# Feed-forward's second layer by 49 block products for 56, and token sums kept in one copy

## The chip, the cores and the metric

The kernel runs on one core of a Trainium2 chip. The metric is the device time in microseconds, as the median of several runs. The profile and trace come from one profiled execution, with its own time.

## The reference, cut to what matters

A gated cross-attention block with a feed-forward network is followed by a slot-pooling block with experts. Batch 8, 512 tokens, width 512. Everything is in 32-bit floats. The change touches the feed-forward network (hidden width 2048) and the preparation of its weights:

```python
xn = layer_norm(x, gamma)
...
h = xn @ Wff1
a, gate = (h[..., :ff_inner], h[..., ff_inner:])
out = out + jax.nn.silu(gate) * a @ Wff2
...
x = x + jnp.tanh(g_xattn[0]) * _L0_xattn_ref(...)
```

Per batch, `xn` (512 x 512) is multiplied by `Wff1` (512 x 4096), and the gated product (512 x 2048) by `Wff2` (2048 x 512).

## The kernel before, in words

Four stages follow one another: cross-attention, the feed-forward network, the expert stage, and the last attention over the slots. Engines run their instructions in the order in which the program issues them (`manual_schedule`), and the order is written out by hand. SP issues nearly all DMAs, and an instruction on its queue that waits for an engine holds up those behind it.

**Seven products for eight.** The feed-forward network multiplies matrices as two by two blocks with seven block products instead of eight, on sums and differences of the blocks. The first layer does this twice, one level inside the other: seven outer products (lists `FIRST`), each of seven inner ones (`INNER`), 49 small products in all. The second layer does it once (`SECOND`), with seven products of eight matmuls each, 56 in all.

**Weights.** The sums of weight blocks are made in cross-attention by the generator `combine_weights`. Its tile `wx` holds four rows of blocks and POOL adds them (L507, helper `op`); SP loads the raw blocks and stores the sums into the DRAM tiles `w1c` and `w2c`. The cross-attention loop runs over half-steps h = 0 to 133 and calls `next(combining, None)` once in each with h > 0 (L818); after the loop, `for _ in combining` would run what is left (L852). For each of two groups `sg`, four `first_layer` calls of 12 steps come before a `second_layer` of 16. In the second layer, ACT scales the raw weights by the gate `tg_x` (L559).

**The feed-forward loop.** k runs over K = 16 pieces of work, two per batch (b = k // 2, sg = k % 2). In each k, `first(k, e, at)` runs for e = 0 to 6 and at = 0 to 6: four matmuls of 128 x 128 x 128 (L1111), then sums out of PSUM by DVE or ACT. Such a step is called a slot here; 49 make a period. PSUM banks: Y (two, in turn), Q, X, R. `moved` copies or adds Y into X (at = 0), tb (at = 2), t_c (at = 4) or the result (at = 6). All these sums pass through `tt` (L933). A later step on Y must wait until Y has been moved out. POOL does part of the work from SBUF: V + Z in e = 5, W + Z and the multiplications of h in e = 6, then four sums of 1024 columns over the hidden blocks (`combine_hidden`, tile `hs`).

`second(k)` is a generator that runs one period behind, from slot 7 of period k + 1. It gives one matmul of 256 columns (L1027) after each slot, two after the one with at = 3, and its results leave PSUM by ops of 512 columns. At the end of the stage the second layer of k = 15 runs alone.

**Tokens.** `xc` holds two copies of the token blocks and their sums, 7 x 7 blocks of 128 columns: one for the batch at work, one for the next, loaded by `load_tokens` (L939) and summed on POOL by `inner_tokens` and `outer_tokens`. `settle(b)` takes statistics of a finished batch on DVE (L1064), normalises on POOL (L1071) and transposes on DVE (L1081). Jobs with a slot number are put into a dictionary by `later`.

**The edge between the stages.** In the last batch, the sums x_kept go out by POOL's queue (L731), the other stores by SP's. SP's first instructions of the feed-forward stage are `load_tokens(0)` and three `load_first` (L964).

## Time and profile before

| quantity | value |
|---|---|
| median of 3 runs | 2792.7 us (2792.15 to 2794.26) |
| the profiled execution | 2795.4 us, span 2793.6 us |
| granted TensorE clock | 0.996 |
| cross-attention | from the start to about 1031 us |
| feed-forward, k = 0 | 1031.9 to about 1077 us |
| feed-forward, 15 periods | about 1077 to 2097 us, 68.0 us each |
| second layer of k = 15 alone | 2097.4 to about 2126.5 us |
| PE busy in 1077 to 2097 | 1019.9 of 1020 us |
| DVE, ACT, POOL busy there | 473.1, 224.9, 565.2 us |

How to read it: an engine's busy time says how long it worked, not whether anything waited for it. In the timelines a row gives the start and the length in us, the engine, the line, the operation with output and inputs, and in brackets the idle time before it and what ended that. A PE row merges records that follow each other, and each 32-bit matmul has two records. Long rows overlap the next ones a little, since a matmul's end includes its way through the array. "L933" is the helper `tt`, so such rows are told apart by tile and shape.

### The profile page before, as it was taken

The page shows a single profiled execution, that of the slowest core. Times are in us where ns is not written, and L with a number is a line of the kernel's source. Part 1 is how long each engine was busy: PE and PEld are TensorE (multiplying, and loading weights), DVE is VectorE, ACT ScalarE, POOL GpSimd, SP SyncE. Part 2 cuts the span into 40 slices and gives each one's busy share as a digit, 9 for nine tenths or more (in the row PEclk, how much of TensorE's full clock was granted, in tenths as well). Part 3 has the DMA queues.
Part 4 walks back from the last instruction along what each step waited for, and adds up shares of the span by engine and source line. Part 5 has one row for each costly group of instructions (what it writes and reads, how often), then busy time and mean ns, then how long its engine had stood idle before and what let it go on. Part 6 is the DMA issues. An engine that isn't in the chain of part 4 may idle for free.

```text
span 2793.6 us, 45441 instructions
## 1 busy us (share of the span) xinstructions
PE 2721.9 (97%) x16826; PEld 1716.7 (61%) x16826; DVE 1529.4 (55%) x3412; ACT 934.4 (33%) x2029; POOL 1442.7 (52%) x1023
## 2 busy tenths in 40 slices
PE   9999999999999999999999999999999998899889
PEld 5333333333333459999999999999997544322233
DVE  7897978888787754444444444444454221111146
ACT  5555556555556542222222222222221222000033
POOL 6787878778787645355555565656552100000035
PEclk9999999999999999999999999999999999999999
DMA  7888878888887788777877787878789799999954
GB/s 233 271 247 239 255 233 244 245 248 238 242 257 218 237 267 314 263 263 257 298 276 287 267 303 250 303 260 307 240 284 350 283 426 423 410 426 427 426 200 153
DMA packets 262973, 794.01 MB, mean 284 GB/s; under 512 B 90912, under 2 KB 121152, under 8 KB 235104
## 3 DMA queue, kind: packets, MB, share of 16 engines
q1 hardware_dynamic: 261872, 788.61, 80.6%
q8 instruction: 134, 2.20, 0.3%
q0 software_dynamic: 640, 2.10, 0.2%
q14 instruction: 87, 0.71, 0.1%
q10 hardware_dynamic: 240, 0.40, 0.0%
HBM read 574.44 MB, written 83.36 MB: 235 GB/s over the span
## 4 chain that ended last, share of the span: by engine, by line
PE 84%; DMA 11%; DVE 3%; ACT 1%; SPq 1%; issue 1%; POOL 0%; DVEq 0%; ACTq 0%; POOLq 0%
PE Y L1111 14%; DMA wg<-in_L_ffn_e_Wg_dram 8%; PE Y L1027 8%; PE av L406 8%; PE sim L327 8%; PE op L420 7%; PE qp L310 7%; PE Z L1027 4%; PE Q L1111 3%; PE R L1111 3%; PE X L1111 3%; PE Q L1027 2%; PE out L1935 2%; PE p_wg L1740 1%; DMA w<-in_L_ffn_e_W_dram 1%; PE pl L1388 1%
## 5 line engine op out<-in xcount | busy, mean ns | idle before, releaser
L354 POOL TENSOR_SCALAR pr<-pr,rden 128x512 f32<-128x512 f32 x378 | 592.2, 1582 | 205.7 <-DVE rden L347 205.4
L341 ACT ACTIVATE pr<-pr,nmx 128x512 f32<-128x512 f32 x512 | 363.4, 711 | 383.2 <-DVE nmx L338 295.6
L1111 PEld LDWEIGHTS Y<-xc,w 128*128 128x128 f32 x3608 | 469.4, 192 | 24.8 <-DVE h L933 0.9
L1111 PE MATMUL Y<-xc,w 128*128 128x128 f32 x3608 | 473.5, 275 | 2.1 <-DVE top_first L933 0.6
L338 DVE CUSTOM_DVE_ANT_0 pr<-sim,bias 128x512 f32<-128x512 f32 x512 | 321.9, 684 | 39.0 <-PE sim L327 39.0
L369 DVE STREAM_TRANSPOSE turned<-pr 128x512 f32<-128x512 f32 x504 | 322.5, 682 | 9.7 <-DMA pT<-turned 1.7
L933 POOL TENSOR_TENSOR fv<-fv,fz 128x512 f32<-128x512 f32 x64 | 79.9, 1269 | 381.3 <-ACT fz L1126 362.5
L327 PE MATMUL sim<-kT,q 64*128 64x512 f32 x1024 | 255.5, 615 | 0.9 <-DVE nmx L338 0.9
L406 PE MATMUL av<-pT,v 128*64 128x512 f32 x1008 | 232.9, 604 | 1.2 <-issue 1.0
L420 PE MATMUL op<-wo,o 128*128 128x512 f32 x512 | 231.3, 594 | 1.4 <-ACT o L412 1.4
L310 PE MATMUL qp<-xnT,wq 128*128 128x512 f32 x496 | 229.3, 605 | 0.5 <-ACT o L412 0.5
L1027 PE MATMUL Y<-w,h 128*128 128x256 f32 x736 | 211.7, 382 | 0.8 <-DVE top_first L933 0.8
L933 DVE TENSOR_TENSOR top_first<-Y,fv 128x512 f32<-128x512 f32 x128 | 88.6, 692 | 183.0 <-PE Y L1111 179.0
L327 PEld LDWEIGHTS sim<-kT,q 64*128 64x128 f32 x1024 | 89.0, 186 | 160.2 <-issue 97.2
L310 PEld LDWEIGHTS qp<-xnT,wq 128*128 128x128 f32 x496 | 89.1, 189 | 135.0 <-issue 119.3
L420 PEld LDWEIGHTS op<-wo,o 128*128 128x128 f32 x512 | 93.5, 190 | 103.2 <-issue 97.1
L406 PEld LDWEIGHTS av<-pT,v 128*64 128x64 f32 x1008 | 67.8, 138 | 141.8 <-issue 118.2
L507 POOL TENSOR_TENSOR wx<-wx 128x512 f32<-128x512 f32 (+2 forms) x96 | 131.0, 1372 | 1.3
L1305 POOL MEMSET cwk<- 128x2048 f32 x1 | 1.8, 1805 | 247.7 <-PE p_w L1740 247.7
L1662 DVE TENSOR_SCALAR place<-tq,vec 128x512 f32<-128x512 f32 x32 | 24.0, 751 | 191.9 <-PE tq L1349 191.9
L1370 POOL TENSOR_SCALAR spr<-spr,ssums 128x512 f32<-128x512 f32 x16 | 25.1, 1571 | 189.1 <-DVE ssums L1369 184.0
L933 DVE TENSOR_TENSOR R<-Q,top_first 128x512 f32<-128x512 f32 x109 | 76.2, 700 | 83.0 <-ACT top_first L1118 78.3
(358 smaller groups left out, 4513.0 us busy)
## 6 DMA issues: line engine op xcount, KB each, us to landing
w<-w1c SPq DMA_DIRECT2D x112, 1792.0 KB, 8.0
w<-in_L_ffn_e_W_dram SPq DMA_DIRECT2D x64, 2048.0 KB, 16.6
pT<-turned SPq DMA_DIRECT2D x1008, 128.0 KB, 2.7
wg<-in_L_ffn_e_Wg_dram SPq DMA_DIRECT2D x32, 2048.0 KB, 27.5
w<-w2c SPq DMA_DIRECT2D x108, 512.0 KB, 8.4
w1c<-wx SPq DMA_DIRECT2D x56, 448.0 KB, 3.6
wq<-wq_kept SPq DMA_DIRECT2D x52, 256.0 KB, 4.8
xn<-in_x_dram SPq DMA_DIRECT2D x32, 256.0 KB, 3.4
```

The costliest lines, as they stand in the source:

```text
L310: nc.tensor.matmul(qp, lhsT=w[:, c, :], rhs=xnT[:, c, :], start=(c == 0), stop=(c == ND - 1))
L327: nc.tensor.matmul(sps[l, e], lhsT=qs[half * HP + l][r, t * P : (t + 1) * P], rhs=kT[r, :], start=True, stop=True,)
L338: nc.vector.tensor_tensor_reduce(pr, sps[l, e], bias, -XSCALE, LARGE, ALU.add, ALU.min, nmx)
L341: nc.scalar.activation(pr, pr, AF.Exp, bias=nmx, scale=-1.0, accum_out=dens[l][:, e : e + 1])
L354: nc.gpsimd.tensor_scalar(prs[l, e], prs[l, e], rden[:, e : e + 1], None, ALU.mult)
L369: nc.vector.transpose(turned[:, :, hd, :].rearrange("p (k j) c -> p k j c", k=4), pr.rearrange("p (j k c) -> p k j c", k=4, c=32),)
L406: nc.tensor.matmul(av[XD * e : XD * e + XD], lhsT=v[:, j, :], rhs=p5[:, j, :, :, e, :], start=(j == 0), stop=(j == NT - 1),)
L420: nc.tensor.matmul(op, lhsT=o[:, l, :], rhs=wo[:, half * HP + l, :], start=(l == 0), stop=(l == HP - 1),)
L507: nc.gpsimd.tensor_tensor(dst, a, b, kind)
L933: eng.tensor_tensor(dst, a, b, op)
L1027: nc.tensor.matmul(bank[:, n], lhsT=h_blocks(k)[pa][:, n, q], rhs=w[:, q], start=fresh[e] and i == 0, stop=True, skip_group_check=True,)
L1111: nc.tensor.matmul(bank[:, q * P : (q + 1) * P], lhsT=w[:, q, ia, :], rhs=x[:, pb, ib, :], start=at < 2 and q == 0, stop=True, skip_group_ ...
```

## The change

The second layer gets the inner level too: seven products of seven inner ones, 49, each of two matmuls of 128 columns. Its weights get the second level in cross-attention: `second_layer(sg, c)` is called twice per sg, with 12 steps each, and `first_layer` has 11 steps instead of 12. `w2c` and the buffers `w2` grow from 8 to 14 blocks of 128 columns per product. The inner sums of the hidden blocks are made on the fly by `combine_inner` into two buffers `gs`, on DVE, four slots ahead of their product; each inner step moves its own 128 columns out of PSUM, and the sums over outer products go to y by `sums`, mostly on POOL.

The tokens have one copy. A row of the next batch's blocks is loaded into the place of a row that the last piece of the batch has just used; `HOLD` says which row lies where, and the jobs' slots are written out by hand. Tiles change their places in SBUF, and a tile `spare` keeps the distance.

```diff
-    w2c = [keep.tile([P, 7 * 1024], F32, name=f"w2c_{sg}") for sg in range(SG)]
+    w2c = [keep.tile([P, 7 * 2 * 7 * P], F32, name=f"w2c_{sg}") for sg in range(SG)]
...
                 put(6, 1)
                 yield
-                yield
-
-            def load(sg, q):
...
-            def first_half(q):
-                w = pieces[q % 2]
-                op(w[:, 4], w[:, 1], w[:, 0], ALU.subtract)
-                op(w[:, 5], w[:, 3], w[:, 4], ALU.subtract)
-
-            def second_half(q):
-                w = pieces[q % 2]
-                op(w[:, 1], w[:, 3], w[:, 1], ALU.subtract)
-                op(w[:, 6], w[:, 2], w[:, 5], ALU.subtract)
...
-            def put_second(sg, q):
-                nc.sync.dma_start(
-                    w2c[sg].rearrange("p (o q d) -> q p o d", o=7, q=4)[q], pieces[q % 2]
-                )
...
-            def second_layer(sg):
-                for i in range(3 * 3 + 6):
...
+
+            def second_layer(sg, c):
+                def put(o, src):
+                    at = (2 * o + c) * 7 * P
+                    nc.sync.dma_start(w2c[sg][:, at : at + 7 * P], o_[src])
...
+                for f in range(2):
+                    for kk in range(2):
+                        nc.sync.dma_start(
+                            wx[:, 2 * f : 2 * f + 2, 2 * kk : 2 * kk + 2].rearrange(
+                                "p h d w -> p h (d w)"
+                            ),
+                            rows_[f, kk],
+                        )
+                yield
+                yield
+                for i in range(2):
+                    raw = wx[:, 2 * i : 2 * i + 2, 0:4].rearrange("p o i w -> p o (i w)")
+                    nc.scalar.activation(raw, raw, AF.Copy, scale=tg_x)
+                yield
+                op(i_[4], i_[1], i_[0], ALU.subtract)
+                op(i_[5], i_[3], i_[4], ALU.subtract)
+                yield
+                op(i_[6], i_[2], i_[5], ALU.subtract)
+                op(i_[1], i_[3], i_[1], ALU.subtract)
+                yield
+                for o in (0, 2, 3):
+                    put(o, o)
+                yield
+                yield
+                op(o_[0], o_[1], o_[0], ALU.subtract)
+                yield
+                put(4, 0)
+                op(o_[1], o_[3], o_[1], ALU.subtract)
+                yield
+                put(1, 1)
+                op(o_[3], o_[3], o_[0], ALU.subtract)
+                yield
+                put(5, 3)
+                op(o_[2], o_[2], o_[3], ALU.subtract)
+                yield
+                put(6, 2)
                 yield
 
             for sg in range(SG):
                 for q in range(4):
                     yield from first_layer(sg, q)
-                yield from second_layer(sg)
+                for c in range(2):
+                    yield from second_layer(sg, c)
 
...
-        xc = [f1.tile([P, 7, 7, P], F32, name=f"xc_{i}") for i in range(2)]
+        xc = f1.tile([P, 7, 7, P], F32, name="xc")
+        HOLD = [[0, 1, 2, 3, 4, 5, 6]]
+        for _ in range(1, B):
+            r = HOLD[-1]
+            HOLD.append([r[0], r[2], r[4], r[5], r[3], r[1], r[6]])
...
+        V, W, Z = (sum_tile(n) for n in ("fv", "fw", "fz"))
         hidden_tile(1)
+        first_tile(1)
+        first_tile(2)
+        w2 = [f1.tile([P, 2, 7, P], F32, name=f"w2_{i}") for i in range(3)]
+        gs = [f1.tile([P, 4, 2, P], F32, name=f"g_{i}") for i in range(2)]
         first_tile(0)
         hidden_tile(0)
-        w2 = [f1.tile([P, 4, HD], F32, name=f"w2_{i}") for i in range(3)]
-        V, W = sum_tile("fv"), sum_tile("fw")
-        first_tile(1)
-        first_tile(2)
-        Z = sum_tile("fz")
         ys_[0] = f1.tile([P, 2, 2, D], F32, name="y_0")
         zs = [[f1.tile([P, HD], F32, name=f"z{i}_{n}") for n in range(2)] for i in range(2)]
+        f1.tile([P, 1664], F32, name="spare")
         hs = f1.tile([P, 3, 2, 4, P], F32, name="hs")
+        ub, u_c = (f1.tile([P, P], F32, name=n) for n in ("ub", "uc"))
...
-        tu, t22 = (top_first[:, i].rearrange("p (n d) -> p n d", n=2) for i in (4, 5))
+        V2, U2 = (top_first[:, i].rearrange("p (n d) -> p n d", n=2) for i in (4, 5))
...
-        Q2 = pf.tile([P, 2, HD], F32, name="Q2")
-        Y2 = pf.tile([P, 2, HD], F32, name="Y2")
-        Z2 = pf.tile([P, 2, HD], F32, name="Z2")
+        Q2, Y2, Z2 = (pf.tile([P, N], F32, name=n) for n in ("Q2", "Y2", "Z2"))
         Y0, Q, X, R = (pf.tile([P, N], F32, name=n) for n in ("Y0", "Q", "X", "R"))
-        others = ((Q, X, R), tuple(t.rearrange("p n d -> p (n d)") for t in (Q2, Y2, Z2)))
+        others = ((Q, X, R), (Q2, Y2, Z2))
...
-        def load_tokens(b):
-            src = xnT_kept[b].rearrange("p (c t n w) -> p c t n w", c=ND, t=2, n=2)
-            for c in range(ND):
-                kk, k2 = divmod(c, 2)
-                nc.sync.dma_start(
-                    xc[b % 2][:, 2 * kk : 2 * kk + 2, 2 * k2 : 2 * k2 + 2, :], src[:, c]
-                )
-
-        def inner_tokens(b, eng, o=slice(0, 4)):
-            x = xc[b % 2][:, o]
+        def load_tokens(b, o):
+            kk, t = divmod(o, 2)
+            src = xnT_kept[b].rearrange("p (c t m) -> p c t m", c=ND, t=2)
+            nc.sync.dma_start(
+                xc[:, HOLD[b][o], 0:4].rearrange("p (c n) w -> p c (n w)", c=2),
+                src[:, 2 * kk : 2 * kk + 2, t],
+            )
+
+        def inner_tokens(b, eng, *os):
+            r = sorted(HOLD[b][o] for o in os)
+            x = xc[:, r[0] : r[-1] + 1 : max(r[-1] - r[0], 1)]
...
-            x = [xc[b % 2][:, o].rearrange("p i n -> p (i n)") for o in range(7)]
+            x = [xc[:, HOLD[b][o]].rearrange("p i n -> p (i n)") for o in range(7)]
...
-            w = hb[0].rearrange("p t f n q w -> p (t f n q w)")[:, 1024 * i : 1024 * i + 1024]
-            return w.rearrange("p (q d) -> p q d", q=4)
+            w = w1[1 + i // 2].rearrange("p q i w -> p (q i w)")
+            n = 2 * 7 * P
+            return w[:, n * (i % 2) : n * (i % 2) + n].rearrange("p (c i d) -> p c i d", c=2, i=7)
...
-                o = SECOND[e][1]
+                o, n = SECOND[e][1], 2 * 7 * P
                 nc.sync.dma_start(
-                    second_weights(c),
-                    w2c[k % SG][:, o * 1024 : (o + 1) * 1024].rearrange("p (q d) -> p q d", q=4),
+                    second_weights(c).rearrange("p c i d -> p (c i d)"),
+                    w2c[k % SG][:, o * n : (o + 1) * n],
...
-        def second(k):
+        def inner_hidden(k, e):
+
+            a = h_blocks(k)[SECOND[e][0]]
+            a11, a12, a21, a22 = (a[:, n, 2 * c : 2 * c + 2] for n in range(2) for c in range(2))
+            a21_, s1, s2, s4 = (gs[(7 * k + e) % 2][:, j] for j in range(4))
+            return [a11, a12, a21_, a22, s1, s2, s4], a21
+
+        def combine_inner(k, e, eng):
+            (a11, a12, a21_, a22, s1, s2, s4), a21 = inner_hidden(k, e)
+            tt(eng, s1, a21, a22, add)
+            tt(eng, s2, s1, a11, sub)
+            tt(eng, a21_, a11, a21, sub)
+            tt(eng, s4, a12, s2, sub)
+
+
+
+        def second(k, e, at):
...
-            banks = (Y2, Q2, Y2, Z2, Y2, Z2, Y2)
-            fresh = (True, True, False, False, False, False, False)
-            v = nc.vector
-            for e, (pa, _) in enumerate(SECOND):
-                if k < K - 1:
-                    load_second(7 * k + e + 2)
-                w, bank = second_weights(7 * k + e), banks[e]
-                for i in range(8):
-                    q, n = divmod(i, 2)
-                    nc.tensor.matmul(
-                        bank[:, n], lhsT=h_blocks(k)[pa][:, n, q], rhs=w[:, q],
-                        start=fresh[e] and i == 0, stop=True, skip_group_check=True,
-                    )
-                    if i == 7:
-                        if e == 0:
-                            tt(v, Z2, Y2, y11, add)
...
-                        elif e == 6:
-                            tt(v, y21, Y2, y21, add)
-                    yield
+            v, s = nc.vector, nc.scalar
+            seed = (None, None, V2, y11, V2, y12, y21)[e]
+            to = (V2, U2, V2, y11, V2, y12, y21)[e]
+            if at == 0 and k < K - 1:
+                load_second(7 * k + e + 2)
+            left, w = inner_hidden(k, e)[0], second_weights(7 * k + e)
+            n = (7 * k + e) % 2
+            bank, both = (Q2, Y2)[n], Z2[:, n * HD : n * HD + HD]
+            Y, Q, X, R = bank[:, 0:P], bank[:, P : 2 * P], both[:, 0:P], both[:, P : 2 * P]
+            ia, ib = SECOND[at]
+            dst = (Y, Q, Y, X, Y, R, Y)[at]
+            for c in range(2):
+                nc.tensor.matmul(
+                    dst, lhsT=left[ia][:, c], rhs=w[:, c, ib], start=at == 0 and c == 0,
+                    stop=True, skip_group_check=True,
+                )
+
+            def moved(dst, n, d):
+                if seed is None:
+                    s.copy(dst, Y)
+                else:
+                    tt(v, dst, Y, seed[:, n, d * P : (d + 1) * P], add)
+
+            if at == 0:
+                moved(X, 0, 0)
+            elif at == 2:
+                moved(ub, 0, 1)
+                tt(v, R, Q, ub, add)
+            elif at == 4:
+                moved(u_c, 1, 1)
+                tt(v, to[:, 1, P : 2 * P], Q, u_c, add)
+            elif at == 5:
+                s.copy(to[:, 0], both)
+            elif at == 6:
+                moved(to[:, 1, 0:P], 1, 0)
+
+        def sums(k, e):
+            y = ys_[(k // SG) % 2]
+            y11, y12, y21, y22 = (
+                y[:, t, :, h * HD : (h + 1) * HD] for t in range(2) for h in range(2)
+            )
+            pairs = (
+                [(y11, V2)], [(y12, U2), (y22, U2)], [(y12, V2)], [], [(y21, V2), (y22, V2)], [], []
+            )[e]
+            return [lambda eng, y=y, a=a: tt(eng, y, y, a, add) for y, a in pairs]
...
-                    bank[:, q * P : (q + 1) * P], lhsT=w[:, q, ia, :], rhs=x[:, pb, ib, :],
+                    bank[:, q * P : (q + 1) * P], lhsT=w[:, q, ia, :], rhs=xc[:, HOLD[b][pb], ib],
...
-        load_tokens(0)
+        for o in range(4):
+            load_tokens(0, o)
...
+        def back(k):
+            at = 49 * (k + 1) + 7
+            for e in range(7):
+                later(at + 7 * e - 4, lambda e=e: combine_inner(k, e, nc.vector))
+                for i in range(7):
+                    later(at + 7 * e + i, lambda e=e, i=i: second(k, e, i))
+                for i, run in enumerate(sums(k, e)):
+                    eng = nc.vector if e == 4 and i == 0 else nc.gpsimd
+                    wait = (1, 8)[e == 4 and i == 1] + i
+                    later(at + 7 * e + 6 + wait, lambda run=run, eng=eng: run(eng))
+
+        RAW = {1: 0, 2: 1, 3: 3, 4: 2}
         hide(0)
-        seconds = []
+        back(0)
         for k in range(1, K):
             b, sg = divmod(k, SG)
             for e in range(7):
                 load_first(7 * k + e + 2)
+                if sg == 1 and b + 1 < B and e in RAW:
+                    load_tokens(b + 1, RAW[e])
+                if k == K - 1 and e > 4:
+                    for i in range(2):
+                        load_second(7 * k + 3 + 2 * (e - 5) + i)
                 for at in range(7):
                     first(k, e, at)
-                    for _ in range(2 if at == 3 else 1):
-                        if seconds and next(seconds[0], "end") == "end":
-                            seconds.pop(0)
-                            if seconds:
-                                next(seconds[0])
                     for run in jobs.pop(49 * k + 7 * e + at, []):
                         run()
-                if e == 0:
-                    seconds.append(second(k - 1))
-                if e == 0 and (sg == 0 or b == 0) and b + 1 < B:
-                    load_tokens(b + 1)
...
                     if b + 1 < B:
-                        for i, run in enumerate(
-                            inner_tokens(b + 1, nc.gpsimd) + outer_tokens(b + 1, nc.gpsimd)
-                        ):
-                            later(49 * k + 10 + 3 * i, run)
+                        inner = inner_tokens(b + 1, nc.gpsimd, 0, 1)
+                        inner += inner_tokens(b + 1, nc.gpsimd, 3, 2)
+                        outer = outer_tokens(b + 1, nc.gpsimd)
+                        runs = [*inner, outer[0], outer[1], outer[3], outer[2]]
+                        for i, run in zip((18, 20, 22, 24, 30, 32, 34, 36, 37, 45, 48, 54), runs):
+                            later(49 * k + i, run)
...
-        for _ in seconds[0]:
-            pass
-        for e in range(2, 7):
-            load_second(7 * (K - 1) + e)
-        for run in combine_hidden(K - 1, nc.vector):
-            run()
-        for _ in second(K - 1):
-            pass
+                back(k)
+        for slot in sorted(jobs):
+            for run in jobs.pop(slot):
+                run()
+        load_second(7 * (K - 1) + 2)
+        k = K - 1
+        outer = combine_hidden(k, nc.vector)
+        combine_inner(k, 0, nc.vector)
+        outer[0]()
+        outer[1]()
+        outer[2]()
+        outer[3]()
+        for e in range(7):
+            if e < 6:
+                combine_inner(k, e + 1, nc.gpsimd)
+            for at in range(7):
+                second(k, e, at)
+            for run in sums(k, e):
+                run(nc.vector)
```

## The prediction

> **What bounds the kernel now.** I read the page first, then the timeline of one feed-forward stretch, then DVE and POOL alone at places where both work on SBUF tiles, then SP and POOL at the end of cross-attention. On the page:
>
> ```profile
> PE 2721.9 (97%) x16826; PEld 1716.7 (61%) x16826; DVE 1529.4 (55%) x3412; ACT 934.4 (33%) x2029; POOL 1442.7 (52%) x1023
> PE 84%; DMA 11%; DVE 3%; ACT 1%; SPq 1%; issue 1%; POOL 0%; DVEq 0%; ACTq 0%; POOLq 0%
> ```
>
> PE is busy throughout and carries the chain. The feed-forward network runs from 1031.9 (first L1111) to 2126.5 us. The windows of it show PE busy 68.00 of 68.00 us in the periods (one per k), so there its time is the matmuls' pitch. The timeline of PE, from at=1 of a product on:
>
> ```profile
> 1603.76 1.05 PE L1111 MATMUL Y<-xc,w 128*128 128x128 f32 x8
> 1604.65 0.60 PE L1027 MATMUL Y<-w,h 128*128 128x256 f32 x2
> 1605.09 1.05 PE L1111 MATMUL X<-xc,w 128*128 128x128 f32 x8
> 1605.98 1.03 PE L1027 MATMUL Y<-w,h 128*128 128x256 f32 x4
> 1606.84 1.05 PE L1111 MATMUL Y<-xc,w 128*128 128x128 f32 x8
> ```
>
> A matmul is two records. Four 128-wide ones take 0.89 us of pitch (1604.65 - 1603.76), so 0.222 each; one 256-wide takes 0.44 (1605.09 - 1604.65). A slot is 1.33 us, the one with two second-layer matmuls 1.75; seven are 9.71, and seven of those the 68.0 of a period.
>
> **PE's gain.** Of each first-layer product's company, 8 matmuls of 256 columns (8 x 0.435 = 3.48) become 14 of 128 (14 x 0.222 = 3.11). That is 0.37 per product, 2.6 per period, 39 us over the 15 periods k = 1 to 15. All of it is on the path. A slot becomes 1.33 everywhere, a period 65.3. The first-layer matmuls and k = 0 stay.
>
> **DVE's new work.** DVE gets, per period, 28 sums of 256 columns in SBUF (`combine_inner`), some 34 ops of 128 columns out of PSUM, and one sum of 512 (y21); six ops of 0.69 go. Nearest rows: 128-wide with PSUM 0.288 (oT<-oT,y_tp), SBUF sums 0.28 at 128 and 1.22 at 1024 columns (hs), on whose line 256 columns take 0.42. So 11.8 + 9.8 + 0.7 - 4.1 = 18 us on top of about 31 busy in 65.3: enough in total. But the order is fixed. The four sums stand in slot 3 of each product, and the next slot's moves out of Y queue behind them. In the trace a tb sum starts 1.16 us after its slot does (Y at 1156.31, sum at 1157.47) and R follows to 1158.90; with two new 0.29 ops the four sums start 3.1 us after slot 2 does. PE's at=6 starts four slots (5.33) after slot 2 and waits for the t_c move (0.69). Room for the four sums: 5.33 - 3.1 - 0.69 = 1.5 us. They need 1.7 undisturbed: a stall near 0.1 each, 0.6 per period. In product 6 another 0.68 op (h<-X,h) is ahead of them, so there some 0.75. Every further us in the four sums is PE's, one for one.
>
> **POOL beside these sums.** This decides. Almost every DVE op of this stage now has one input in PSUM. Where DVE adds SBUF to SBUF beside POOL, at the start of the stage and at its end, the trace shows (DVE, then POOL; then POOL and DVE at 2100):
>
> ```profile
> 1031.87 0.29 DVE L933 TENSOR_TENSOR xc<-xc 128x128 f32<-128x128 f32 x1
> 1032.28 1.10 DVE L933 TENSOR_TENSOR xc<-xc 128x128 f32<-128x128 f32 x1
> 1033.62 0.70 DVE L933 TENSOR_TENSOR xc<-xc 128x128 f32<-128x128 f32 x1
> 1034.24 0.81 DVE L933 TENSOR_TENSOR xc<-xc 128x128 f32<-128x128 f32 x1
> 1034.97 0.82 DVE L933 TENSOR_TENSOR xc<-xc 128x128 f32<-128x128 f32 x1
> ...
> 1032.49 0.74 POOL L933 TENSOR_TENSOR xc<-xc 128x256 f32<-128x256 f32 x1
> 1033.30 0.87 POOL L933 TENSOR_TENSOR xc<-xc 128x256 f32<-128x256 f32 x1
> 1034.13 0.78 POOL L933 TENSOR_TENSOR xc<-xc 128x256 f32<-128x256 f32 x1
> 1034.86 0.78 POOL L933 TENSOR_TENSOR xc<-xc 128x256 f32<-128x256 f32 x1
> ```
>
> ```profile
> 2100.02 2.49 POOL L933 TENSOR_TENSOR h<-h,fv 128x512 f32<-128x512 f32 x2
> 2101.91 1.67 DVE L933 TENSOR_TENSOR hs<-h 128x1024 f32<-128x1024 f32 x1
> ```
>
> A 0.28 op takes 0.70 to 1.10, and each ends 0.14 to 0.15 after a POOL op ends (1033.38 after 1033.23; 1034.32 after 1034.17; 1035.05 after 1034.91; 1035.79 after 1035.64). The long one ends 1.07 after its POOL op, 0.15 less than its 1.22 alone. So the DVE sum stands until POOL's running op is done, then runs, and POOL's next op is in before DVE's next. The lower bound is 0.5 us lost per sum, as in these rows whatever POOL runs; the upper is the whole POOL op each time. I take the upper, since the ends follow POOL's ends for 0.74 and for 1.25 us ops alike.
>
> What POOL runs in slot 3 of the products is in its timeline around k = 3's start (1212.8):
>
> ```profile
> 1210.89 1.27 POOL L933 TENSOR_TENSOR h<-h,fw 128x512 f32<-128x512 f32 x1
> 1214.69 2.50 POOL L933 TENSOR_TENSOR h<-h,fv 128x512 f32<-128x512 f32 x2
> 1217.14 2.35 POOL L933 TENSOR_TENSOR hs<-h 128x1024 f32<-128x1024 f32 x1
> 1224.20 2.35 POOL L933 TENSOR_TENSOR hs<-h,hs 128x1024 f32<-128x1024 f32 x1
> ```
>
> It is busy without a gap from 53 us into a period (V+Z) to 13.7 us into the next. So:
> - product 6 (60 us in): four sums against 1.25 us ops: 0.6 for the first, three more of 1.25 less what overlaps, 3.5 lost, with the 0.75 above 4.2 us;
> - product 0 (5.7 us in): against the 2.35 us ops and the new y22 sum (1.27): 5.7 to 14.3 instead of 7.4, then a `to` sum and u_c, for which second at=6 was due at 8.9: 6.2 us. Queued behind them are the moves of both layers, and PE waits for these in order;
> - product 2 of the even periods from k = 4: POOL's four norms (2.08 each, L1071) now meet slot 17: 4 us in 6 periods;
> - odd periods: token sums in place (2.09 at slots 37 and 45, the small ones after a load that lands 8.9 us after issue, as xc's did) and 0.86 us of stats in slot 17: some 3 us in 7 periods;
> - 0.6 per period as above.
> Sum: 15 x (6.2 + 4.2 + 0.6) + 6 x 4 + 7 x 3 = 165 + 24 + 21 = 210 us.
>
> A rule of the Trainium skill (SBUF — State Buffer, Who interferes with whom) speaks against the change: it says that a DVE instruction with two SBUF inputs contends with a GpSimd one that reads SBUF, and that the later of the two fully blocks. By that rule the sum is the 210 above; without it, by the 0.5 us of the short rows, it is the 103 of the first rival.
>
> **The end of cross-attention.** `combine_weights` had 128 steps for 133 calls; now 8 x 11 + 4 x 12 = 136, so the last pieces come after the loop. POOL's last sums stand behind the last store of x_kept, and on SP the last three puts, which wait for them, stand ahead of the first loads of tokens and w1. Now:
>
> ```profile
> 1014.48 2.12 SPq L939 DMA_DIRECT2D xc<-xnT_kept  x4
> 1031.93 0.54 POOL L731 DMA_DIRECT2D x_kept<-xr  x1 [7.49 <-DVE xc L933]
> ```
>
> The two scalings (1.15 each) now stand in call 127 ahead of ACT's copy of o, which delays the rest by about 2.3: the store ends at 1034.8, three sums of 2.1 end at 1041.1, the last put goes, four token loads (2.1) take SP to 1043.8, then w1 lands 8.0 later: 1051.8. The first matmul was at 1031.9. That is 20 us of idle PE. Bounds: 2 us (POOL's sums early after all) to 25 (the next two w1 late too). In the loop itself I take +1: the batches' kp matmuls are 124.0 apart with first-layer sums of 2.1 us on POOL and 124.6 and 125.5 around the second layer's; bounds -2 and +4.
>
> **The rest, at nothing or nearly.** Loads: 896 KB for 512 per product, 18.8 MB per period over some 80 us, 235 GB/s; the windows show 258 to 293 now at a DMA share of 0.68 to 0.84, later slices 426. Cover: three buffers, two products (19 us) ahead, 8.4 to landing; gone, it would cost the difference per product, some 3 us. ACT's new copies: 15 of 68 us busy now. The last second layer, 2097.4 to 2126.5: 98 x 0.222 = 21.8 plus moves of 0.29 between steps, sums of 0.69 and POOL's 24 small sums in contention: 24 to 32, I take -2.
>
> **Sum.** -39 + 210 + 20 + 1 - 2 = +190 against the profiled execution's 2795.4 (span 2793.6): 2985. That execution lies 2.7 above the median of the runs: 2983.
>
> **Rivals.**
> 1. The lock costs only the 0.5 us per sum of the short rows: 2.0 in product 0, 2.75 in product 6, 0.8 for norms, 0.7 for odd periods, 0.6: 6.9 per period, 103. For it: those are the measured excesses. Against: the ends follow POOL's. -39 + 103 + 20 - 1 = +83: 2876.
> 2. Faster: DVE's sums find gaps in POOL's queue (PE's own stalls let POOL run ahead) and PE keeps its 65.3. Then -39 + 20 - 1 = -20, 2773; with the boundary hidden too, 2755. It decides below (39 - 20 + 1) / 15 = 1.3 us of stall per period. For it: DVE's total fits. Against: POOL has no gap at products 6 and 0.
> 3. The products do not get cheaper: small matmuls at more than 0.222 through the waits between them. At 0.25, 98 x 0.028 = 2.7 per period eats the 39; by itself no change, with the rest 3023. Against: k = 0's 128-wide stretches run at 0.222.
>
> **How the numbers follow.** About 0.2% (5.6 us) is what a measurement can tell from no change. Forecast with its bounds (2900 to 3060): 0.66. Rival 1 (2830 to 2900): 0.17. Rival 3: 0.04. Faster: 0.10; stalls of 1 to 1.7 us per period, no change: 0.03. Slower then 0.87. 2845 to 3060 leaves out the two good cases, an edge of rival 1 and of the top.
>
> **What would show it.** Right: `combine_inner`'s sums at 1.3 to 2.6 us instead of 0.42 in products 6 and 0; PE idle before L1111 and the second layer's matmuls, released by DVE; periods near 79; SP's first xc load after 1035. Wrong: sums near 0.42 all along, periods near 65.3, or PE waiting for POOL or a DMA rather than DVE.

## The result, and the profile after

The changed kernel takes 3086.9 us (median, 3084.7 to 3090.1) against 2792.4 for the kernel before: 1.1055 times as long, 95% interval 1.1036 to 1.1074. It is slower, as forecast, but by 294 us and not by 190; the range (2845 to 3060) does not hold it. The profiled execution has a span of 3083.5 us, 289.9 more than before.

The two lines of the page that answer to those shown of before:

```profile
PE 2791.7 (91%) x18170; PEld 1796.6 (58%) x18170; DVE 1912.2 (62%) x4305; ACT 980.9 (32%) x2237; POOL 1615.4 (52%) x1150
PE 67%; DVE 16%; DMA 11%; issue 3%; ACT 1%; SPq 1%; POOL 1%; DVEq 0%; ACTq 0%; POOLq 0%
```

DVE now carries 16% of the chain of work instead of 3%. (In the changed kernel first-layer matmuls are L1153, second-layer ones L1056, all sums L942.) The windows tell where. First the kernel before, k = 1 to 15 and then the last second layer alone (the tail); then the changed kernel. The columns are stretch, length, busy time of PE, PEld, DVE, ACT and POOL, the granted clock, DMA share and GB/s:

```profile
1079.20:2097.10 1017.90, 1017.77 (x7543) 973.57 (x7542) 470.94 (x748) 224.93 (x390) 563.19 (x366) 1.00 0.78 277
2097.10:2126.50 29.40, 28.62 (x134) 24.91 (x133) 10.45 (x12) 2.66 (x4) 6.52 (x7) 1.00 0.91 332
```

```profile
1105.60:2358.00 1252.40, 1070.21 (x8789) 1036.25 (x8789) 843.92 (x1596) 268.34 (x584) 687.77 (x471) 0.96 0.72 260
2358.00:2417.70 59.70, 41.27 (x232) 36.45 (x232) 24.02 (x58) 5.50 (x17) 24.89 (x30) 0.77 0.69 252
```

PE, which had no idle time in the periods, has 182 us of it (1252.4 - 1070.2), and its clock is no longer full. The parts of the 289.9:

| part | forecast | measured |
|---|---|---|
| first matmul | +21 | +23.7 (1031.9 to 1055.6) |
| k = 0 | 0 | +2.7 (47.3 to 50.0) |
| k = 1 to 15 | -39 + 210 = +171 | +234.5 (1017.9 to 1252.4) |
| tail | -2 | +30.3 (29.4 to 59.7) |
| after it | 0 | -1.3 |

**What was forecast and is there.** DVE and POOL in product 6, k = 9 (four `combine_inner` sums, then POOL beside them):

```profile
1848.95 0.89 DVE L942 TENSOR_TENSOR g<-h 128x256 f32<-128x256 f32 x1
1849.88 1.37 DVE L942 TENSOR_TENSOR g<-g,h 128x256 f32<-128x256 f32 x1
1851.17 1.48 DVE L942 TENSOR_TENSOR g<-h 128x256 f32<-128x256 f32 x1
1852.58 1.48 DVE L942 TENSOR_TENSOR g<-h,g 128x256 f32<-128x256 f32 x1
...
1849.51 1.45 POOL L942 TENSOR_TENSOR fw<-fw,fz 128x512 f32<-128x512 f32 x1
1851.04 1.33 POOL L942 TENSOR_TENSOR h<-h,fw 128x512 f32<-128x512 f32 x1
1852.34 1.44 POOL L942 TENSOR_TENSOR fw<-fw,fz 128x512 f32<-128x512 f32 x1
```

The second to fourth sums end at 1851.25, 1852.65 and 1854.06, each 0.28 to 0.29 after a POOL op ends (1850.96, 1852.37, 1853.78): each stands until POOL's running op is done, then runs. The four take 5.1 us; undisturbed they take 1.55 (1231.91 to 1233.46 in k = 2). So 3.6 are lost (forecast 3.5).

**What was not forecast.** What PE waited for in k = 1 to 15, by the waits view (total, times, longest):

```profile
PE Z L1056 <- DVE Z L942: 71.2, 104, 1.5
PE Y L1153 <- DVE top_first L942: 43.9, 16, 2.8
PE Q L1056 <- DVE y L942: 15.7, 4, 5.1
PE Y L1056 <- DVE y L942: 13.6, 4, 4.6
PE Q L1056 <- DVE top_first L942: 11.3, 4, 3.5
PE Y L1056 <- DVE top_first L942: 10.2, 4, 3.9
```

The second line is the lock's stall in product 6, about once per period and 2.7 us each (43.9 / 16). The next four (50.8) are, but for 1.2 us, the one in product 0: 14 times, 2.97 to 5.13 us, 3.5 on average. The first line is another wait, and the largest: it is there in every product. In the timeline of a product with no slow sum it looks so (PE, then DVE):

```profile
1230.30 1.06 PE L1153 MATMUL X<-xc,w 128*128 128x128 f32 x8
1232.15 0.68 PE L1056 MATMUL Z<-w,hs 128*128 128x128 f32 x4 [0.79 <-DVE Z L942]
...
1230.05 0.69 DVE L942 TENSOR_TENSOR top_first<-Y,fv 128x512 f32<-128x512 f32 x1 [1.78 <-PE Y L1153]
1230.78 0.70 DVE L942 TENSOR_TENSOR R<-Q,top_first 128x512 f32<-128x512 f32 x1
1231.39 0.28 DVE L942 TENSOR_TENSOR ub<-Y,top_first 128x128 f32<-128x128 f32 x1
1231.70 0.30 DVE L942 TENSOR_TENSOR Z<-Y,ub 128x128 f32<-128x128 f32 x1
```

The second layer's at=3 matmul goes into X's columns of bank Z2. X was moved in long before (1227.98); what it waits for is the write into R's columns beside them, R's move (end 1232.00). Whether the chip needs that order, or only the program's bookkeeping asks for it, no run here separates. The move stands behind the first layer's tb and R. And after most of the long waits PE runs at half pace for a while (timeline of PE at the end of k = 9, then the window of the half pace, columns as above):

```profile
1854.71 1.16 PE L1153 MATMUL Y<-xc,w 128*128 128x128 f32 x8 [2.76 <-DVE top_first L942]
1855.96 0.71 PE L1056 MATMUL Y<-w,hs 128*128 128x128 f32 x4
1856.51 1.86 PE L1153 MATMUL Y<-xc,w 128*128 128x128 f32 x8
1858.17 1.06 PE L1056 MATMUL Q<-w,h 128*128 128x128 f32 x4
...
1856.57:1859.98 3.41, 3.41 (x18) 3.41 (x18) 1.03 (x3) 0.57 (x1) 3.41 (x4) 0.50 0.95 324
```

The eight records of 1856.51 take 1.66 to the next start (1858.17), where 0.89 is usual; the granted clock is 0.50 there.

### The profile page after: what moved, and what is told of

The parts are those of the page before. It is cut to its first block, busy times and chain, and to the rows that moved or that the text cites. A ratio compares the mean times of both kernels' runs of the same rounds, so it can differ in the third digit from the quotient of the medians.

```text
span 3083.5 us, 49706 instructions
## 1 busy us (share of the span) xinstructions
PE 2791.7 (91%) x18170; PEld 1796.6 (58%) x18170; DVE 1912.2 (62%) x4305; ACT 980.9 (32%) x2237; POOL 1615.4 (52%) x1150
## 4 chain that ended last, share of the span: by engine, by line
PE 67%; DVE 16%; DMA 11%; issue 3%; ACT 1%; SPq 1%; POOL 1%; DVEq 0%; ACTq 0%; POOLq 0%
PE Y L1153 11%; DMA wg<-in_L_ffn_e_Wg_dram 7%; PE sim L327 7%; PE av L406 7%; PE op L420 7%; PE qp L310 6%; DVE g L942 5%; PE Q L1056 4%; PE Y L1056 3%; PE Z L1056 3%; PE Q L1153 3%; DVE top_first L942 3%; DVE R L942 2%; PE R L1153 2%; PE out L1999 1%
## 5 line engine op out<-in xcount | busy, mean ns | idle before, releaser
L1153 PE MATMUL Y<-xc,w 128*128 128x128 f32 x3608 | 496.3, 283 | 64.4 <-DVE top_first L942 44.5
L1153 PEld LDWEIGHTS Y<-xc,w 128*128 128x128 f32 x3608 | 457.4, 199 | 68.7 <-DVE top_first L942 47.7
L420 PE MATMUL op<-wo,o 128*128 128x512 f32 x512 | 231.4, 595 | 2.8 <-ACT o L412 2.8
L942 POOL TENSOR_TENSOR fv<-fv,fz 128x512 f32<-128x512 f32 x64 | 79.8, 1266 | 189.0 <-ACT fz L1168 162.6
L505 POOL TENSOR_TENSOR wx<-wx 128x512 f32<-128x512 f32 (+1 forms) x96 | 161.9, 1692 | 17.1 <-DMA pT<-turned 7.5
L942 DVE TENSOR_TENSOR top_first<-Y,fv 128x512 f32<-128x512 f32 x128 | 88.0, 687 | 125.5 <-PE Y L1153 121.0
L942 POOL TENSOR_TENSOR xc<-xc 128x256 f32<-128x256 f32 (+1 forms) x92 | 111.2, 1223 | 100.0 <-DMA xc<-xnT_kept 45.6
L420 PEld LDWEIGHTS op<-wo,o 128*128 128x128 f32 x512 | 93.5, 190 | 104.9 <-issue 97.3
L942 POOL TENSOR_TENSOR y<-y,top_first 128x512 f32<-128x512 f32 x40 | 51.2, 1286 | 160.6 <-ACT top_first L1063 106.1
L942 DVE TENSOR_TENSOR R<-Q,top_first 128x512 f32<-128x512 f32 x109 | 76.2, 699 | 90.8 <-ACT top_first L1160 87.1
L425 DVE SCALAR_TENSOR_TENSOR xr<-op,gates,xr 128x512 f32<-128x512 f32 x64 | 47.9, 748 | 134.8 <-PE op L420 134.8
```

The lines of the kernel that those rows point to most:

```text
L420: nc.tensor.matmul(op, lhsT=o[:, l, :], rhs=wo[:, half * HP + l, :], start=(l == 0), stop=(l == HP - 1),)
L505: nc.gpsimd.tensor_tensor(dst, a, b, kind)
L942: eng.tensor_tensor(dst, a, b, op)
L1153: nc.tensor.matmul(bank[:, q * P : (q + 1) * P], lhsT=w[:, q, ia, :], rhs=xc[:, HOLD[b][pb], ib], start=at < 2 and q == 0, stop=True, skip ...
```

## The experiments

Lengths of the seven products of k = 9, from the starts of the first layer's matmuls in each trace, and the stretch k = 1 to 15:

| kernel | products 0 to 6 (us) | period | k = 1 to 15 |
|---|---|---|---|
| before | 9.7 9.9 9.7 9.7 9.7 9.7 9.7 | 68.1 | 1017.9 |
| changed | 14.7 10.4 10.1 10.4 10.4 10.2 14.8 | 81.0 | 1252.4 |
| e1_moves_first | 15.1 11.3 9.8 10.4 9.7 9.8 16.1 | 82.0 | |
| e2_no_sums | 10.2 10.4 10.1 10.4 10.4 10.2 11.3 | 73.1 | 1110.2 |
| e5_one_input | 10.2 10.4 10.1 10.4 10.4 10.2 11.4 | 73.1 | 1101.3 |
| e7_one_input_moves_first | 9.5 9.9 9.6 9.7 9.7 9.5 10.9 | 68.7 | 1035.0 |
| e6_late_hidden | 10.6 10.3 10.1 12.5 10.4 10.2 15.0 | 79.2 | |
| e8_combined | 9.5 9.8 9.8 10.3 9.7 12.3 10.6 | 72.0 | |
| e9_combined_2 | 9.5 11.6 9.8 11.4 9.7 9.5 9.8 | 71.3 | 1064.9 |

### Do the sums cost, and is it the lock? (e2, e5)

```
 e2:  if 7 * k + e < 2:  later(..., combine_inner(k, e, nc.vector))
 e5:  for dst, src in ((s1, a21), (s2, a11), (a21_, a22), (s4, a12)):
          nc.vector.transpose(dst, src)          # instead of four tt(...)
```

> Leaves out combine_inner's four sums in all products but the first two of k=0 and those of the last k, so the weights meet old sums; everything else stays. Theory L (prediction: the sums cost through POOL's lock): the waits of 3.0 to 3.5 us in product 0 and 2.8 in product 6 go, and with them the half-clock stretches after them (2.4 to 5.4 us per period by the matmuls' pitch): 8 to 11 per period, 120 to 165 in 15: 2945 (2920 to 2970); the waits of 0.45 to 0.86 before at=3 stay, periods near 72. Rival M (the 34 new 128-wide moves in DVE's queue, not the sums, make the waits): above 3050.

> Each of combine_inner's four sums (all but those of the last k) is replaced by a transpose of one block of 256 columns into the same place: 0.42 us on DVE like an undisturbed sum, but with one SBUF input instead of two; the combined blocks are therefore not formed. Theory L (lock between DVE's two SBUF inputs and POOL): the transposes take 0.42 everywhere, as L1123's do, product 0 and 6 keep under 1 us of stall each, and the time is near that without the sums, 2950 (2925 to 2975). Rival Q (the sums' own place in DVE's queue, whatever their inputs): the waits of about 3 us in products 0 and 6 stay: 3060 to 3090.

e2: 2938.2 (ratio 1.0519, 1.0503 to 1.0535). e5: 2931.1 (1.0492, 1.0476 to 1.0507). The sums cost some 150 us; and four DVE instructions of the same place and length, but with one SBUF input, cost none of it. So it is the lock and not the sums' share of DVE's queue. Nor is it the operation: the same TENSOR_TENSOR with one input in PSUM, `top_first<-Y,fv`, takes 687 ns on average in the changed kernel and 692 before, though POOL is busy for over half of the time. The groups of e5 by form (busy, mean ns), and then those of the changed kernel:

```profile
L1033 DVE STREAM_TRANSPOSE g<-h 128x256 f32<-128x256 f32 x240 | 84.8, 411 | 0.0
L1033 DVE STREAM_TRANSPOSE g<-hs 128x256 f32<-128x256 f32 x180 | 63.6, 410 | 0.9 <-POOL hs L942 0.9
```

```profile
L942 DVE TENSOR_TENSOR g<-h 128x256 f32<-128x256 f32 x122 | 117.3, 961 | 0.0
L942 DVE TENSOR_TENSOR g<-g,h 128x256 f32<-128x256 f32 x61 | 64.4, 1056 | 2.1
```

0.41 beside the same POOL work where the sums took 0.96 and 1.06. e5's windows split the 151 us of k = 1 to 15 (1252.4 - 1101.3):

```profile
1108.50:2209.80 1101.30, 1017.29 (x8790) 991.92 (x8790) 682.87 (x1598) 268.23 (x584) 666.95 (x469) 1.00 0.81 294
```

PE's idle time falls from 182 to 84: 98 us were stalls. Its busy time falls from 1070.2 to 1017.3 at the same number of matmuls, and the clock is 1.00 again: 53 us were, nearly all, PE at half pace after the stalls (a mean clock of 0.96 over 1252.4 us is worth some 50). e2 lies 7 above e5; its k = 1 kept the sums of the first two products, and that period takes 78.5 against 69.7.

### The wait at at=3 (e1, e7)

```
 at == 2, first layer:  moved(tb, 0, 1)
-                       tt(v, R, Q, tb, add)
+                       last_move.append(lambda: tt(v, R, Q, tb, add))   # run after the slot's second-layer moves
```

> Same arithmetic; in each slot at=2 DVE's first-layer sum R<-Q,tb is issued after the second layer's two moves (ub, then R's half of bank Z2) instead of ahead of them. Theory A, read from the trace of the changed kernel: in every product PE stands 0.45 to 0.86 us before the second layer's at=3 matmul (X's half of Z2) until DVE has written R's half of the same bank, and that write stands behind the first layer's tb and R sums (0.69 and 0.70); 4.5 us per period in all, of which about 4 go: 15 x 4 = 60, so 3027 (3010 to 3045), and products 2 to 5 fall from 10.1 to 11.1 us to about 9.5. Theory B, the prediction's own steps (only DVE's sums beside POOL in products 0 and 6 cost, 0.6 per period for the rest): at most 9 less, 3078 to 3090.

> e5_one_input (2931; the sums replaced by transposes, the combined blocks not formed) with the order of e1_moves_first: the second layer's two moves of slot at=2 ahead of the first layer's R. Theory A (the 0.45 to 0.86 before at=3 in each of seven products is the second layer's own chain behind tb and R, and e1 gained only 21 because the lock then took more): without the lock all of it shows, 15 x 4.5 = 67 less than e5: 2866 (2855 to 2885), periods 68 to 69 instead of 73.1 and 74.4. Theory B (the wait only changes its place, as e1's 21 suggest): 2905 to 2931.

e1: 3066.0 (1.0975, 1.0958 to 1.0991), 21 less than the changed kernel and neither theory's number. Products 2, 4 and 5 of the table fell by 0.3 to 0.7, but products 0, 1 and 6 rose, product 6 from 14.8 to 16.1, so that k = 9 takes even longer than in the changed kernel; the 21 us come from the even periods (k = 10: 82.5 for 86.2). Over the stretch the wait before Z is gone, and the waits before the first layer's Y grew from 43.9 to 52.4: what DVE saves ahead of its sums is largely spent beside POOL again. So e1 alone could not price the wait. e7, the same edit on e5, does: 2866.5 (1.0255, 1.0239 to 1.0271), 65 below e5 where 67 was expected, with every product 0.5 to 0.7 shorter. Its windows:

```profile
1103.80:2138.80 1035.00, 1011.92 (x8790) 993.80 (x8788) 670.24 (x1597) 268.62 (x584) 666.20 (x468) 1.00 0.85 313
```

### Moving POOL's long sums (e6)

```
-zip(combine_hidden(k, nc.gpsimd), (0, 3, 5, 8))
+zip(combine_hidden(k, nc.gpsimd), (5, 11, 18, 25))
```

> Same arithmetic; POOL's four sums of combine_hidden (2.35 us each) are issued in slots 5, 11, 18 and 25 of the next period instead of 0, 3, 5 and 8, so that POOL has no long sum running in slot 3 of product 0. Theory L (lock): product 0 falls from 14.7 to 16.1 us to 10.4 to 11, product 6 stays; 15 x 4.5 to 5.5: 3012 (2995 to 3040). Rival Q (DVE's queue): no change, 3075 to 3090.

3068.8 (1.0976, 1.0956 to 1.0995): 18 of the 75 hoped for. In odd periods product 0 fell to 10.6 to 11.8 and product 3, where a moved sum now meets DVE's, rose from 10.4 to 12.5; in even ones product 0 stayed at 15.3 and more. The slot in which an instruction is issued is not when POOL runs it: with the token sums ahead of them in the queue, the first two hidden sums still fall beside DVE's (POOL, then DVE, k = 8):

```profile
1691.67 2.55 POOL L942 TENSOR_TENSOR hs<-h 128x1024 f32<-128x1024 f32 x1
1694.29 2.41 POOL L942 TENSOR_TENSOR hs<-hs,h 128x1024 f32<-128x1024 f32 x1
...
1692.04 2.46 DVE L942 TENSOR_TENSOR g<-g,h 128x256 f32<-128x256 f32 x1
1694.42 2.56 DVE L942 TENSOR_TENSOR g<-h 128x256 f32<-128x256 f32 x1
```

The stall goes where POOL's sums go, which is the lock again; as a repair it is worth little.

### The end of cross-attention (e3)

```
 put(6, 2)        # second-layer pieces
-yield
 put(6, 1)        # first-layer pieces
-yield
+if sg:
+    yield
```

> Eight of combine_weights' yields taken out (the last one of each second-layer piece and of the first four first-layer pieces): 128 steps again for 133 calls, nothing else changed. Theory (prediction's boundary term of 20): the last puts are through before the loop ends, SP issues the token loads as early as in the kernel before, first L1153-like matmul near 1034 instead of 1055.6: 3066 (3060 to 3072). Rival: the two scalings in ACT and cross-attention's later end make most of it: first matmul after 1045, 3076 to 3087.

3062.7 (1.0960, 1.0941 to 1.0978), 24 less; the two profiled spans differ by 20.2, of which 14.8 are the earlier first matmul (1055.6 to 1040.8). SP's queue in the changed kernel and PE's idle time behind it:

```profile
1021.92 22.35 SPq L549 DMA_DIRECT2D w2c<-wx x7
1044.37 2.23 SPq L947 DMA_DIRECT2D xc<-xnT_kept x4
1055.59 2.04 PE L1153 MATMUL Y<-xc,w 128*128 128x128 f32 x8 [18.48 <-DMA w<-w1c]
```

and in e3:

```profile
1023.73 4.46 SPq L947 DMA_DIRECT2D xc<-xnT_kept x4
1036.06 3.70 PE L420 MATMUL op<-wo,o 128*128 128x512 f32 x8 [0.74 <-ACT o L412]
1040.82 1.05 PE L1153 MATMUL Y<-xc,w 128*128 128x128 f32 x8
```

With the puts out of the way SP's token loads start 20.6 us earlier, and the idle time is gone. But the first matmul stands at 1040.8, not 1034: it now follows cross-attention's own last matmuls (L420) at once, and these end 9 us later than in the kernel before (5 in the changed kernel). That the longer work on the second layer's weights takes this time is likely and not shown.

### The tail (e4, e10)

```
 e4:  steps = sorted((4 * e + at, e, at) for e in range(7) for at in range(7))
      for i, e, at in steps:  second(k, e, at)     # own[e]: combined blocks in V, W, Z
 e10: no combine_hidden, no combine_inner for the last k
```

> Same arithmetic; the last k's second layer alone: product e+1's steps start at product e's at=4 instead of after it, the outer sums stand between steps of product 0, the combined blocks lie in V, W and Z (free by then), so that no sum waits for a buffer. Theory T (the tail's 59.7 us are PE's waits for each step's moves, 0.81 and 0.26 and more per product, 5.4 for the outer sums in DVE's queue, and half clock after them): the tail takes 30 to 38 and the kernel 3063 (3055 to 3072). Rival (the sums beside each other on DVE and POOL bound the tail): above 50 us, 3078 to 3090.

> The changed kernel without the last k's combine_hidden and combine_inner sums, so its second layer meets old blocks; everything else stays. It tells what of the 59.7 us tail is the sums: if they make it (5.4 us of outer sums in DVE's queue, POOL's inner sums beside DVE's, waits for a free buffer), 30 to 38 and the kernel 3063 (3055 to 3070); if it is the second layer's own chain of moves (0.81, 0.26 and 0.55 us before steps 3, 6 and the next product) with PE's half clock, 45 to 53 and the kernel 3077 (3070 to 3085).

e4: 3076.2 (1.1005, 1.0987 to 1.1022), tail 50.1. e10: 3074.8 (1.1008, 1.0990 to 1.1027), tail 50.2. So the sums are 9.5 of the 30 lost; the other 21 are the second layer's own chain and the clock (granted 0.90 in e10's tail, 0.77 in the changed kernel's). One product of e10:

```profile
2382.33 1.16 PE L1056 MATMUL Q<-w,g 128*128 128x128 f32 x8 [0.94 <-DVE Z L942]
2384.30 0.68 PE L1056 MATMUL Z<-w,h 128*128 128x128 f32 x4 [0.81 <-DVE Z L942]
2384.82 0.61 PE L1056 MATMUL Q<-w,g 128*128 128x128 f32 x4
2385.26 0.61 PE L1056 MATMUL Z<-w,g 128*128 128x128 f32 x4
2386.14 0.71 PE L1056 MATMUL Q<-w,h 128*128 128x128 f32 x4 [0.26 <-DVE top_first L942]
```

A product takes 5.4 us (2382.33 to 2387.76) for 14 matmuls worth 3.1. Between the third and the fourth step stand two dependent moves, ub and R, and PE waits 0.81 for them, not 0.29. Two products interleaved (e4), with all the sums in, also come to 50.1, far from the 30 to 38 expected. Its window shows 36.5 us of busy PE at a clock of 0.83, so 13.6 idle; what holds e4 there was not separated further.

### All of it together (e8, e9)

```
 e8: e1 + e3 + e4; combine_inner of products 0, 1, 6 on POOL, the others on DVE in slot 1;
     W+Z products, combine_hidden, norms, outer token sums issued later
 e9: e8 with POOL's y and token sums and norms shifted again, product 5 of even periods on POOL,
     y21 one slot later; in the tail (3.5 * e + at, e, at)
```

> Same arithmetic; e1, e3 and e4 together, and the lock avoided: the inner sums of products 0, 1 and 6 on POOL, in its own order, the others on DVE in slot 1 of their product (product 2: slot 3); W+Z and its products, the hidden sums, the norms and the outer token sums issued where DVE has no two-input sums. If the causes named so far (lock 8 to 12 per period with its half clock, at=3 4.5 per period, tail 30, boundary 15 to 20) are all, periods come to 66 to 69 and the kernel to 2800 (2765 to 2870). If POOL becomes the bound (its sums 0.7 to 0.8 each, 12 of them, in a stretch that is busy already): PE waits for POOL in products 0 and 1, 2870 to 2960.

> Same arithmetic; e8_combined (2911) with what its trace still showed taken out: the waits of 2.7 us at product 3 of even periods and product 5 of odd ones (DVE's sums beside POOL's norms, y sums and token sums, or waiting for s4 queued behind token sums) by other slots for those POOL sums, product 5's inner sums of even periods on POOL, the y21 sum one slot later than Z's move; in the tail two products strictly alternate (one starts 3.5 steps after the other) and the first inner and outer sums go in beside the last steps of the product before. If nothing but lock, move order, tail and boundary stands between the changed kernel and the kernel before: periods 66.5 to 68, tail 32 to 40, 2800 (2785 to 2830); PE's saving of 2.6 per period is then about eaten by the moves. If POOL's queue is the bound by now, some products stay at 11 and more: 2850 to 2910.

e8: 2910.6 (1.0408, 1.0387 to 1.0428), the time of its second case but not for the reason given there: PE's longest waits are still for DVE's Z (51.6 us over the stretch), at products 3 and 5, where DVE's sums met POOL's moved ones. e9: 2868.1 (1.0266, 1.0249 to 1.0283), not the 2800 expected but in its second case (2850 to 2910). That case's sign is there, products of 11 and more (1 and 3 in k = 9); its reason, POOL's queue, is not what the waits show. e9 gives 219 of the 294 us back and does not beat the kernel before. What PE waits for in its k = 1 to 15:

```profile
PE Y L1158 <- DVE top_first L942: 14.8, 20, 2.4
PE Z L1059 <- DVE Z L942: 7.6, 6, 2.8
PE Q L1059 <- DMA w<-w2c: 6.7, 5, 2.7
```

The lock is still met here and there, loads of the second layer's weights come too late five times, and the tail is still 48.1.

## Why the prediction was right or wrong

**Direction, mechanism: right.** The lock was named as what decides, and e5 shows it: some 150 us go when the same DVE work has one SBUF input. The rule of the Trainium skill (SBUF — State Buffer, Who interferes with whom), that the later of the two is blocked for the whole instruction, agrees with the ends 0.28 after POOL's; so does its other half, that a DVE instruction with one SBUF input does not contend, with the 0.41 of e5. Beside POOL's norms, which read SBUF too, the sums did not stand (see the norms' term), so there the measurement decides against the rule as it is worded. Rival 1 (0.5 us per sum) falls: a sum in product 6 lost 0.9 on average (3.6 / 4), and the lock's whole price, 151, lies between this rival's 103 and the forecast. Rival 2 falls: PE stood idle 12 us per period (182 / 15), not under 1.3. Rival 3 falls too: outside the waits and the half pace the small matmuls keep their 0.222 (two of them from 2384.82 to 2385.26 in e10's lines, 0.44).

**The lock's term (201 of the 210, without the 0.6 per period): too high, and of other make.** Measured 151. The sums were lengthened as forecast (3.6 lost for 3.5 in product 6; in product 0 of k = 10 they ran from 1863.66 to 1870.43, 6.8 us for the 8.6 forecast). But PE's stalls in these products were 2.7 and 3.5, not 4.2 and 6.2, and all idle time that went with the lock is 98 us. The other 53 are PE at half pace after them, which the forecast had at nothing.

**The norms' 4 us per even period: the size came out, by luck, and the cause did not.** Late even periods take 86.2 and odd ones 81.0, but product 2, where the norms meet the sums, takes 10.1 in both, and the sums there are not lengthened (POOL, then DVE, k = 10):

```profile
1887.42 6.50 POOL L1113 TENSOR_SCALAR top_first<-top_first,mvy,rsy 128x512 f32<-128x512 f32 x3
...
1890.51 0.41 DVE L942 TENSOR_TENSOR g<-hs 128x256 f32<-128x256 f32 x1
1890.96 0.42 DVE L942 TENSOR_TENSOR g<-g,hs 128x256 f32<-128x256 f32 x1
1891.30 0.42 DVE L942 TENSOR_TENSOR g<-hs 128x256 f32<-128x256 f32 x1
1891.63 0.42 DVE L942 TENSOR_TENSOR g<-hs,g 128x256 f32<-128x256 f32 x1
```

Of the 30 sums that began beside a norm in this kernel, 29 took 0.41 to 0.43 and one 0.74. So DVE stands for POOL's TENSOR_TENSOR here, but not for a norm of 2.1 us. Of the 5.2 between k = 9 and k = 10, products 0 and 1 make 3.5 (16.1 and 12.5 for 14.7 and 10.4): product 0's stall is 3.5 in k = 10 and 3.0 in k = 9, and half pace goes with it in k = 10 alone (clock 0.50 from 1870.22 to 1877.05). Products 3 and 4 make 1.4, which are in e5 as well (its periods take 74.4 and 73.1). The 3 us of the odd periods were not priced by a run of their own.

**The steps that failed: "0.6 per period as above", and "all of it is on the path".** For the room of the sums the forecast followed only the first layer's at=6 and its t_c move. It gave the second layer's 128-wide moves time on DVE but never asked which second-layer matmul waits for them. That is at=3, which waits for R's move in every product: 66 us (1101.3 - 1035.0) where the step had 9. The second step is the matmuls' saving, which the next paragraph takes up. The excess of k = 1 to 15 over the forecast, 63, is 57 for the wait and 56 for the saving that did not come, less 50 for the lock's term. With the tail's 32 that is nearly all of the 100 by which the whole was missed.

**PE's gain (-39): there in the pitch, not in the time.** Without lock and without that wait, e7 still takes 1035.0 for k = 1 to 15, 17 more than before, where -39 was due. The pitch of its 8790 records is 980 (0.1115 each by their starts, half of the 0.222 per matmul). The other 55 are pauses: the windows show 23 as idle time (1035.0 - 1011.9), for DVE's Z and ACT's fw among others; the rest does not show as idle, as rows overlap the next ones a little, and no run tells what it is. The kernel before had 0.1 us of idle time in the same stretch, so the smaller matmuls leave PE waiting for moves even in the best order tried.

**The tail: wrong by 32.** "Moves of 0.29 between steps" should have been the whole way from PE's matmul through two dependent moves back to PE, 0.81, and 5.4 us per product for the 3.1 of the matmuls. The contention of the sums, which the forecast did name, is only 9.5 of it.

**The boundary: right.** The puts ahead of SP's loads were forecast at 20, the idle time is 18.5. The loop's +1 was too small: 5 in the changed kernel (23.7 - 18.5), 9 in e3.

**Loads and ACT at nothing: right** in the changed kernel, where no such wait is among the large ones; e9's 6.7 us for w2c show that a load can come late in another order. It is not PE's pace alone: e7 is faster through k = 1 to 15 and has no such wait.

## What to carry to other kernels

When a matmul is cut into smaller ones, go through every one of the new matmuls and ask which move it waits for, and what stands ahead of that move in the engine's queue; the cost is the way there and back, not the move's own duration. Beside a POOL that is busy with sums, give DVE work in forms with one SBUF input where that is possible (0.41 for about 1 us per op here), or let POOL do the sums itself in its own order (e9's products 0 and 6 take 9.5 and 9.8 so); issuing POOL's sums elsewhere mostly moved the stall. The matmuls' saving, forecast at 39 us or 4%, was smaller than the lock's 151 or the wait's 66, so first look for the wait that will eat it.

## What was not expected of the hardware

Most of PE's stalls near 3 us are paid twice: PE then runs at half pace for 3.4 or 6.8 us (granted clock 0.50 from 1856.57 to 1859.98, after the wait of 2.76, and from 1870.22 to 1877.05, in and after the wait of 3.52). In k = 1 to 15 that made nearly all of the 53 us on top of 98 of stalls; the changed kernel's tail has a granted clock of 0.77. The Trainium skill (TensorE: Matmul & The Clock Gate, Part 1) tells of such a gate, which halves the clock after an idle window of about 3.4 us; here a wait of 2.76 us was enough, and before it PE had been busy but for waits of under 1 us. The length of the wait does not decide alone: in k = 9 product 0's wait of 2.97 (to 1789.66) has no half pace after it (clock 1.00 from 1789.70 to 1795.00).

POOL's own ops grew too: its `fw<-fw,fz` sums take 1457 ns on average in the changed kernel and 1271 before. But they take 1378 in e2, without DVE's sums, so at most 80 of the 186 go with these; where the rest comes from stays open.
